# First layer: the last subchunk's convolutions on both column halves of the array

## The chip, the core and the metric

The kernel runs on one core of a Trainium2 chip. The core has a matrix engine (TensorE, PE in the profile; its weight loads are PEld), VectorE (DVE), ScalarE (ACT), GpSimd (POOL) and a queue engine, SyncE (SP), which here issues DMAs. Matmuls write to PSUM, an accumulator memory of 128 partitions, and only VectorE and ScalarE read it here. The metric is the time of one execution on the device, in microseconds; the time before is the median of three runs. The profile is of one more execution, which has a time of its own.

## What is computed

The input is 8 images of 56 x 56 pixels with 192 channels, float32. Four layers follow one another, each of the form x + layer(groupnorm(x)). The change touches the first, a gated Toeplitz convolution over rows and columns with 576 inner channels:

```
p = silu(x @ p_w.T + p_b)
q = silu(x @ q_w.T + q_b)
v = silu(x @ v_w.T + v_b)
qv = q * v
o1 = toeplitz(qv along a row,    a1)     # per channel, length 56
o2 = toeplitz(qv along a column, a2)
out = (p * (o1 + o2)) @ o_w.T + o_b
```

The tables a1 and a2 (112 values for each channel) come from two small MLPs over positions and a decay. The other layers are a windowed outlook attention, a gated attention unit and a recurrent scan; their code is the same before and after.

## The kernel before

**Tiling of the first layer** (`layer0`, line 136 on). The 576 inner channels are 9 subchunks of DS = 64 channels, numbered n = 9 b + s over the images b. Two subchunks make a chunk c; the last chunk, c = 4, has only one, s = 8, which the code calls the tail. Per image the loop at line 613 runs over the chunks.

**A subchunk's way.** `project` (line 283) forms q and v by matmuls over 7 image rows at a time in four steps g; ScalarE applies silu (line 310), and `multiply` (line 316) writes their product into the tile `qv`, on VectorE (line 319) and, partly transposed, on POOL and for the last step also on VectorE (line 325). `turn` (line 342) transposes qv on TensorE (line 352) and copies the outcome into the tiles `left` (`ol`, by VectorE) and `right` (`or`, by ScalarE), both at line 359. The other rows of these two tiles hold Toeplitz matrices of the channels, which `toeplitz` (line 265) loads for subchunk n + 2 when the convolutions of n are done, in four DMAs of 16 channels a side (line 275). `convolve` (line 363) then needs one matmul for each channel d, at line 376: 120 rows of `left` and `right` give the 56 x 56 sum o1 + o2 of that channel.

**The array's halves.** One such product has 64 columns of weights, half of the array's 128. For the ordinary subchunks a step q alternates between u = 0 and u = 1, so that channel d goes to PSUM partitions 0 to 63 and channel d + 32 to partitions 64 to 127; two steps of 32 products, with one copy of 120 partitions each into the tile `ot`. For the tail a step has u = 0 alone: four steps of 16 products on partitions 0 to 63, with one copy of 56 partitions each. Copies alternate: VectorE at line 392 for even q, ScalarE at line 390 for odd q. The tail's `ot` is laid out as [56, 56, 64], with the channel innermost.

**What follows the tail.** `post_tail` (line 491) forms the gate p of the last 64 channels (lines 503 and 510), transposes `ot` back (line 524), multiplies (line 530), applies the output matrix (lines 537 and 549) and adds into the accumulators (line 401). Its steps are mixed (`merge`, line 591) with the transposes `turn` of the next image's first two subchunks. Beside the tail's convolutions come the four steps of the next image's `project`, put ahead of them.

**Order and buffers.** In this layer the order on TensorE is the program's (`manual_schedule`, line 604); the other engines' queues are ordered by the compiler framework from dependencies. PSUM is used through `banks()` (line 159): a ring of four tiles of two banks each (line 157), so a step can start once the readers of the tile four steps back are done.

Of the kernel before, what the change touches and what calls it, by code (L numbers as in the profile page):

```python
# [17 lines left out]
H = 56  # L18
# [117 lines left out]
def layer0(cx, xin, xout, w, consts):  # L136
# [6 lines left out]
    tc, nc = cx.tc, cx.nc  # L143
# [7 lines left out]
    with ExitStack() as es:  # L151
# [7 lines left out]
        def banks():  # L159
            return cx.tile(psc, [128, 2, 512], "c")  # L160
# [22 lines left out]
        with ExitStack() as pes:  # L183
# [22 lines left out]
            for t in (1, 2):  # L206
# [13 lines left out]
                for i in range(3):  # L220
                    ps = banks()[0:32, 0, 0:NP]
# [4 lines left out]
                for s in range(NS):  # L226
                    ps = banks()[0:DS, 0, 0:NP]
# [135 lines left out]
        def convolve(n, ot):  # L363


            s = n % NS
            left, right = pairs[n % 2]
            tail = s == NS - 1

            def step(q):  # L370
                ps = banks()
                for k in range(2):
                    for v in range(8):
                        for u in range(1 if tail else 2):
                            d = q * 16 + 8 * k + v + u * 32
                            nc.tensor.matmul(  # L376
                                ps[u * 64 : (u + 1) * 64, k, v * H : (v + 1) * H],
                                left[:, d * H : d * H + 64],
                                right[:, d * H : (d + 1) * H],
                                start=True, stop=True, skip_group_check=True,  # L380
                            )
                if tail:
                    dst = ot[0:H, :, q * 16 : q * 16 + 16].rearrange("p h (k v) -> p h k v", k=2)
                    src = ps[0:H, :, 0 : 8 * H].rearrange("p k (v h) -> p h k v", h=H)
                else:
                    d0 = s % 4 * 32 + 16 * q
                    dst = ot[:, d0 : d0 + 16, :].rearrange("p (k v) h -> p k (v h)", k=2)
                    src = ps[0:120, :, 0 : 8 * H]
                if q % 2:
                    nc.scalar.copy(dst, src)  # L390
                else:
                    nc.vector.tensor_copy(dst, src)

            return [lambda q=q: step(q) for q in range(4 if tail else 2)]

        def add(m, j, x, ps):

# [213 lines left out]
        for b in range(B):  # L611
            more = b + 1 < B
            for c in range(NC):
# [17 lines left out]
                if c % 2 == 0:  # L631
                    ot = cx.tile(cp, [120, 128, H] if two else [H, H, DS], "ot")
                ahead = project(xn, c + 1) if two else project(nxt, 0) if more else []
                convs = []
                for m in (n, n + 1) if two else (n,):
                    *some, last = convolve(m, ot)
                    convs += some + [lambda m=m, last=last: (last(), toeplitz(m + 2))]
# [1397 lines left out]
```

## Time and profile before

| what | value |
|---|---|
| median of three runs | 4327.92 us (4323.49 to 4331.09) |
| the profiled execution | 4314.29 us, span 4312.5 us |
| mean granted TensorE clock | 0.975 |
| line 376, convolutions of the first layer | 9216 matmul records, 313.9 us of TensorE busy time |
| line 352, transposes of qv | 4032 records, 283.8 us |
| lines 294 and 301, projections | 2304 records, 428.8 and 233.2 us |
| copies of the tail, lines 392 and 390 | 16 on VectorE, 1080 ns each; 16 on ScalarE, 900 ns each |
| VectorE and ScalarE, share of the span | 54% and 41% |

How to read it: a busy time is the union of the intervals in which instructions of that group are in the engine, so overlapped matmuls count once; the mean duration of one is longer (223 ns at line 376), since their pipelines overlap. Each float32 product shows as two records; a transpose at line 352 shows as one. Eight images with 9 subchunks of 64 products make the 9216 records. In a list of groups or of the timeline, `out<-in` names the tiles, then partitions x elements, and the bracket holds the idle time before the instruction and what ended it.

### The profile page before, as it was taken

What the parts mean: (1) busy time and instruction counts of PE and PEld (TensorE: products, weight loads), DVE (VectorE), ACT (ScalarE), POOL (GpSimd) and SP (SyncE); (2) the same over time, 40 slices, a digit from 0 to 9 for tenths busy, and PEclk for the clock granted to TensorE, in tenths of its full rate; (3) what the DMA queues carried; (4) which work ended last, traced back from release to release, by engine and by line L of the source; (5) the groups of instructions that cost most, each with busy time, mean ns of one, the idle gap of its engine ahead of it and who ended that gap; (6) DMA issues with size and microseconds to landing.
All of it is one profiled execution on the core that took longest, in us unless ns stands there. A gap on an engine that the chain in (4) does not pass through costs nothing. (4 is left out here: it accounts for less than half of the span.)

```text
span 4312.5 us, 106542 instructions
## 1 busy us (share of the span) xinstructions
PE 4073.2 (94%) x46380; PEld 2680.7 (62%) x46380; DVE 2334.9 (54%) x3429; ACT 1782.9 (41%) x2052; POOL 1512.1 (35%) x1295
## 2 busy tenths in 40 slices
PE   6999999999999999999789999869998999998997
PEld 4666767676676666767456666524444555555997
DVE  4546555454656446554444444356665766664664
ACT  2334434334443343444234434223334555554664
POOL 3222232222322222232133333133333444444776
PEclk9999999999999999999889999879999999999999
DMA  6755242242523225232224344455547776664233
GB/s 137 142 106 142 61 113 61 70 104 61 133 71 98 53 69 128 61 94 73 72 65 116 97 107 104 126 165 171 171 140 175 170 177 154 156 152 113 76 111 93
DMA packets 379607, 484.14 MB, mean 112 GB/s; under 512 B 175780, under 2 KB 324372, under 8 KB 377236
## 3 DMA queue, kind: packets, MB, share of 16 engines
q1 hardware_dynamic: 373636, 466.97, 42.6%
q10 hardware_dynamic: 5504, 10.35, 0.8%
q8 instruction: 365, 5.98, 0.6%
q14 instruction: 102, 0.84, 0.1%
HBM read 321.49 MB, written 155.65 MB: 111 GB/s over the span
## 5 line engine op out<-in xcount | busy, mean ns | idle before, releaser
L325 POOL TENSOR_TENSOR qv<-s,s 128x392 f32<-128x392 f32 (+3 forms) x320 | 567.8, 1796 | 1471.8 <-ACT s L310 1471.5
L359 ACT COPY or<-c 56x1024 f32<-56x1024 f32 (+1 forms) x288 | 256.3, 901 | 442.7 <-DVE ol L359 433.1
L310 ACT ACTIVATE s<-c,bqv 128x784 f32<-128x784 f32 (+1 forms) x320 | 278.4, 911 | 378.5 <-PE c L301 184.2
L294 PE MATMUL c<-xa,wqv 128*128 128x392 f32 x1152 | 428.8, 513 | 4.3 <-DVE xa L49 2.7
L319 DVE TENSOR_TENSOR qv<-s,s 128x784 f32<-128x784 f32 (+1 forms) x160 | 200.8, 1255 | 261.2 <-ACT s L310 261.2
L359 DVE COPY ol<-c 56x1024 f32<-56x1024 f32 (+1 forms) x288 | 300.0, 1077 | 63.8 <-PE c L352 62.5
L376 PEld LDWEIGHTS c<-or,ol 120*64 120x64 f32 x9216 | 305.4, 138 | 37.2 <-issue 27.3
L376 PE MATMUL c<-or,ol 120*64 120x56 f32 x9216 | 313.9, 223 | 9.4 <-DMA ol<-ed 7.8
L294 PEld LDWEIGHTS c<-xa,wqv 128*128 128x128 f32 x1152 | 209.0, 192 | 174.6 <-issue 35.3
L352 PEld LDWEIGHTS c<-ident,qv 64*120 64x120 f32 x4032 | 257.3, 138 | 55.4 <-issue 35.1
L352 PE MATMUL c<-ident,qv 64*120 64x64 f32 x4032 | 283.8, 224 | 3.8 <-POOL qv L325 2.5
L1367 PE MATMUL v<-wvb,wa 128*128 128x512 f32 (+1 forms) x400 | 193.0, 615 | 49.2 <-ACT wa L1278 30.0
L301 PE MATMUL c<-xb,wqv 64*128 64x392 f32 x1152 | 233.2, 518 | 0.0
L427 ACT ACTIVATE s<-c,bp 128x448 f32<-128x448 f32 x224 | 129.9, 631 | 246.9 <-PE c L420 246.9
L1900 POOL TENSOR_TENSOR y<-y,s 128x448 f32<-128x448 f32 x168 | 185.1, 1102 | 93.1 <-ACT s L1879 93.1
L1869 PE MATMUL h<-ringv,am 128*64 128x57 f32 (+1 forms) x4400 | 192.6, 235 | 19.7 <-DVE ringv L1856 12.7
L458 PE MATMUL c<-po,wo 128*128 128x448 f32 x448 | 198.1, 564 | 7.0 <-DVE po L447 7.0
L1869 PE MATMUL h<-ringh,am 128*64 128x57 f32 (+1 forms) x4400 | 186.1, 231 | 8.8 <-DVE ringh L1875 8.8
L1378 ACT ACTIVATE vb<-sm 128x1024 f32<-128x1024 f32 (+1 forms) x100 | 103.7, 1038 | 214.2 <-issue 187.2
L413 PE MATMUL c<-xa,wp 128*128 128x224 f32 x896 | 190.3, 355 | 0.0
L401 DVE TENSOR_TENSOR acca<-c,acca 128x392 f32<-128x392 f32 (+1 forms) x120 | 67.3, 586 | 219.0 <-PE c L463 204.8
L1869 PEld LDWEIGHTS h<-ringv,am 128*64 128x64 f32 x4400 | 168.1, 140 | 23.0 <-DVE ringv L1856 13.6
(219 smaller groups left out, 7583.6 us busy)
## 6 DMA issues: line engine op xcount, KB each, us to landing
or<-tt SPq DMA_DIRECT2D x252, 196.0 KB
ol<-tt SPq DMA_DIRECT2D x252, 196.0 KB
vt<-v SPq DMA_DIRECT2D x56, 672.0 KB
v<-vb SPq DMA_DIRECT2D x96, 384.0 KB
x<-x SPq DMA_DIRECT2D x112, 168.0 KB
x<-x SPq DMA_DIRECT2D x112, 112.0 KB
bt<-bs SPq DMA_DIRECT2D x28, 448.0 KB
bs<-bs SPq DMA_DIRECT2D x56, 224.0 KB
```

The lines of the kernel that those rows point to most:

```text
L294: nc.tensor.matmul(ps[:, h, 0:n], wqv[0][:, j, :], xn[0][:, at : at + n], start=True, stop=False,)
L301: nc.tensor.matmul(ps[:, h, 0:n], wqv[1][rows, j, :], xn[1][rows, g * n : (g + 1) * n], start=False, stop=True,)
L310: nc.scalar.activation(t, ps[rows, :, 0:n], AF.Silu, bias=bqv[rows, j : j + 1])
L319: nc.vector.tensor_tensor(sub(qv[rows, 7 * g :, 64 + H - 1 :], (HH * 120, 2), (120, 7), (-1, H)), *(t.rearrange("p u (h w) -> p u h w", w= ...
L325: eng.tensor_tensor(sub(qv[rows, w0:, H - 1 - 7 * g - HH * u :], (120, w1 - w0), (-1, 7)), *(t[:, u].rearrange("p (h w) -> p w h", w=H)[:, ...
L352: nc.tensor.transpose(view(i // 8)[:, :, i % 8], qv[e : e + DS, i0 + i, :], ident[e : e + DS, e : e + DS],)
L359: copy(dst, src[rows])
L376: nc.tensor.matmul(ps[u * 64 : (u + 1) * 64, k, v * H : (v + 1) * H], left[:, d * H : d * H + 64], right[:, d * H : (d + 1) * H], start=Tr ...
L413: nc.tensor.matmul(out(u, h), wp[0][:, 2 * j + u, :], xn[0][:, at : at + n], start=(u == 0), stop=True, skip_group_check=True,)
L458: nc.tensor.matmul(pa, wo[:, 2 * j + u, 0:CA], pos[u], start=(u == 0), stop=(u == 1))
L1367: nc.tensor.matmul(out, x[:, at : at + n], wt, start=(k == 0), stop=(k == 1), skip_group_check=True,)
L1869: nc.tensor.matmul(ps[sides[c], y], am[a][:, m * CB : (m + 1) * CB], old[:, x], start=(n < 2), stop=True, skip_group_check=True,)
```

## The change

In the tail, a step's 32 products now alternate between both column halves, as in the ordinary subchunks, and there are two steps where there were four. Step q computes channels 16 q to 16 q + 15 on PSUM partitions 0 to 63 and channels 32 + 16 q to 47 + 16 q on partitions 64 to 127. The tile `ot` keeps its layout on partitions 0 to 55, so each step ends with two copies of 56 partitions: VectorE copies the lower half to where it was, and ScalarE copies the upper half from partitions 64 to 119 to partitions 0 to 55. Nothing is changed for the ordinary subchunks.

```diff
@@ -371,7 +371,7 @@
                 ps = banks()
                 for k in range(2):
                     for v in range(8):
-                        for u in range(1 if tail else 2):
+                        for u in range(2):
                             d = q * 16 + 8 * k + v + u * 32
                             nc.tensor.matmul(
                                 ps[u * 64 : (u + 1) * 64, k, v * H : (v + 1) * H],
@@ -380,8 +380,12 @@
                                 start=True, stop=True, skip_group_check=True,
                             )
                 if tail:
-                    dst = ot[0:H, :, q * 16 : q * 16 + 16].rearrange("p h (k v) -> p h k v", k=2)
-                    src = ps[0:H, :, 0 : 8 * H].rearrange("p k (v h) -> p h k v", h=H)
+                    for u, copy in enumerate((nc.vector.tensor_copy, nc.scalar.copy)):
+                        d0 = q * 16 + u * 32
+                        dst = ot[0:H, :, d0 : d0 + 16].rearrange("p h (k v) -> p h k v", k=2)
+                        src = ps[u * 64 : u * 64 + H, :, 0 : 8 * H]
+                        copy(dst, src.rearrange("p k (v h) -> p h k v", h=H))
+                    return
                 else:
                     d0 = s % 4 * 32 + 16 * q
                     dst = ot[:, d0 : d0 + 16, :].rearrange("p (k v) h -> p k (v h)", k=2)
@@ -391,7 +395,7 @@
                 else:
                     nc.vector.tensor_copy(dst, src)
 
-            return [lambda q=q: step(q) for q in range(4 if tail else 2)]
+            return [lambda q=q: step(q) for q in range(2)]
```

## The prediction

> **What bounds the kernel now.** I read the page's first two parts, then the waits of TensorE inside layer 0, then the timeline around the last subchunk's convolutions, and then the same stretch of time in each image. The page first: busy time of each engine, then the span in 40 slices.
>
> ```profile
> PE 4073.2 (94%) x46380; PEld 2680.7 (62%) x46380; DVE 2334.9 (54%) x3429; ACT 1782.9 (41%) x2052; POOL 1512.1 (35%) x1295
> ...
> PE   6999999999999999999789999869998999998997
> PEclk9999999999999999999889999879999999999999
> ```
>
> TensorE (PE) is busy 94% of the span, and layer 0, which ends near 2116 us (slices 1 to 20), shows nines after its first slice. Next, who TensorE waits for inside layer 0 (70 to 2116 us; total, times, longest):
>
> ```profile
> PE c L376 <- DMA ol<-ed: 7.8, 1, 7.8
> PE c L458 <- DVE po L447: 7.0, 8, 0.9
> PE c L537 <- DVE s L530: 3.3, 6, 2.1
> PE c L549 <- ACT or L359: 2.9, 5, 0.6
> ```
>
> These and three smaller rows make 26.3 us in 2046. So in this layer TensorE's own sequence is the time, and a matmul that goes saves its slot as long as nobody else becomes late. Now the timeline of the stage that changes, in image 0 (start, duration, engine, line, operation, count, idle before it):
>
> ```profile
> 319.91 7.67 PE L376 MATMUL c<-or,ol 120*64 120x56 f32 x128
> 321.17 0.53 DVE L325 TENSOR_TENSOR qv<-s,s 128x196 f32<-128x196 f32 x1 [3.35 <-ACT s L310]
> 321.61 1.66 DVE L319 TENSOR_TENSOR qv<-s,s 128x784 f32<-128x784 f32 x1
> 323.19 1.20 DVE L325 TENSOR_TENSOR qv<-s,s 128x196 f32<-128x196 f32 x1
> 323.88 0.90 ACT L390 COPY ot<-c 56x896 f32<-56x896 f32 x1 [2.75 <-PE c L376]
> 324.32 1.07 DVE L392 COPY ot<-c 56x896 f32<-56x896 f32 x1
> 327.51 1.15 PE L352 MATMUL c<-ident,qv 64*120 64x64 f32 x16
> 328.70 1.22 DVE L359 COPY ol<-c 56x1024 f32<-56x1024 f32 x1 [1.87 <-PE c L352]
> 329.95 1.01 ACT L359 COPY or<-c 56x1024 f32<-56x1024 f32 x1 [1.44 <-DVE ol L359]
> 332.08 2.35 DVE L359 COPY ol<-c 56x1024 f32<-56x1024 f32 x2 [2.15 <-PE c L352]
> 332.83 1.03 PE L524 MATMUL c<-ident,ot 56*128 56x56 f32 x14
> 337.05 1.04 DVE L401 TENSOR_TENSOR acca<-c,acca 128x392 f32<-128x392 f32 x2 [1.75 <-PE c L537]
> ```
>
> The tail's 64 products (128 records: each float32 product leaves two) take from 319.91 to 327.51, and TensorE then goes on at once. The price of both forms, from the busy table of four stretches (length; busy time and count of PE, weight load, VectorE, ScalarE and POOL; granted clock; DMA share and GB/s): two tails, the four steps of two ordinary subchunks, and one lone ordinary step:
>
> ```profile
> 319.91:327.51 7.60, 7.60 (x130) 7.54 (x129) 5.32 (x5) 2.12 (x3) 3.61 (x3) 1.00 0.47 127
> 2093.42:2100.87 7.45, 7.45 (x129) 7.45 (x129) 2.16 (x2) 0.90 (x1) 0.00 (x0) 1.00 0.01 2
> 364.59:372.20 7.61, 7.61 (x258) 7.55 (x257) 5.38 (x5) 2.14 (x3) 3.78 (x3) 1.00 0.64 172
> 494.45:496.45 2.00, 2.00 (x66) 1.94 (x64) 0.00 (x0) 1.97 (x3) 0.00 (x0) 1.00 0.08 26
> ```
>
> The third stretch has 256 records of the same operand shape in the time in which the tail has 128: products that alternate between the two column halves cost half each. The trace has eight tails, of 7.60 us to the next instruction in seven images and 7.45 in the last.
>
> [...] the ordinary steps need 7.61 / 256 = 30 ns a record, the tail 7.60 / 128 = 59 ns. [...] here copies are 1.08 us (VectorE) and 0.90 us (ScalarE), before as after. [...] at 328.70 VectorE copies one half of a tile's partitions, ScalarE's copy of the other half starts at 329.95, just after VectorE's end at 329.92, and is put down to it. I take that order for the two new copies of one tile as well.
>
> **The change part by part.**
> (1) Products. Nothing goes and nothing is added: 64 products, 128 records an image. The order moves so that the two column halves alternate, 4 steps of 16 becoming 2 of 32. At 30 ns a record that is 128 x 7.61 / 256 = 3.81 us where 7.60 were. Gain 3.79 us in seven images and 7.45 - 3.81 = 3.64 in the last: 26.5 + 3.6 = 30.2 us. Bounds: the lone steps' 2.00 us each would make 4.00 us, a gain of 28.6 us; the record spacing without the change-over to the next line is nowhere under 29 ns, so no more than 31.
> (2) Copies. Still two on VectorE and two on ScalarE an image, of 56x896 each; what moves is when and in which order. Half of them now shift from partitions 64 up to 0 up. No copy of this line does that before; the nearest is L310, where ScalarE reads the upper 64 partitions of a tile and writes the lower: 911 ns for 64x784, the same as the 128x784 form. I take nothing; at worst the shift costs as much again, 0.90 us on ScalarE, which is covered as (3) shows.
> (3) The chain behind them, in image 0's clock. TensorE's two steps end at 321.8 and 323.72. VectorE is in its qv products until 324.39 in any case (if it takes a copy in between, they end 1.08 us later and the sum is the same). Its copies then end at 325.47 and 326.55, ScalarE's at about 326.4 and 327.5. TensorE goes on 3.79 us sooner: the first transposes (L352) at 323.72, the gate (L503, L510) at 324.81, two more transpose steps at 327.09 and 328.1, and the tail's back-transposes (L524) at 329.04. What each needs: the first transposes read rows 0 to 15 of qv, whose writers are VectorE's first product, done at 321.7, and the first of POOL's two (2.74 us together from 321.28), done near 322.65; the tile they take is freed by ScalarE's activations, done at 321.14. The second transpose step takes the tile of the first convolution step, free at 326.4 against 327.09, and qv, done at 324.4; the third the tile of the second, free at 327.5 against 328.1. L524 needs ot, ready at 327.5, and the tile of the first transposes: VectorE copies that at 326.55 to 327.77, ScalarE until 328.8, against 329.04. Every margin is positive but small, 0.2 to 0.7 us. I take 0.05 us an image for semaphores and bound it by 0 and 1 us.
> (4) What VectorE finds next. It arrives 1.7 us late against TensorE's new clock, and the rows above show its idle times before that matters: 1.87 us at 328.70, 2.15 at 332.08 and 1.75 at 337.05. The lateness is gone by the second; from 337 on VectorE is busy to 364 without a pause of note, so without those gaps all of the gain would be in danger.
> (5) Toeplitz loads (L275, on SP). Tail steps free the columns d in another order: 0 to 15 and 32 to 47 after step one, the rest after step two. The loads are queued 0, 16, 32, 48, so the second waits for step two; all eight issues are then through at about 326 where it was 328.35. They serve the convolution of subchunk 10, some 40 us on: nothing. The image loads and stores behind them on SP hang on the same TensorE sequence and come 3.8 us earlier too.
> (6) Last image: no project step beside the tail. TensorE ends at 2097.2, copies at 2099.4, L524 would start at 2099.4: a stall of 0.1 at most. Layer 1 starts with loads that follow the last stores, which follow these sums, so it moves as a whole. Layers 1 to 3 hold the same instructions.
> Sum: 30.2 - 8 x 0.05 = 29.8, say 30 us. The profiled execution (4314.29 us, its span 4312.5) becomes 4284.3; the median shown, 13.6 us above it, 4327.9 - 30 = 4298.
>
> **The rivals.**
> *A, half the gain stays in the copies.* If VectorE and ScalarE are ordered worse than in (3), for instance strictly one after the other over all four copies, ot is ready at 324.39 + 2 x (1.08 + 0.90) = 328.35 and the first transposes' tile, at the back of that queue, at 330.6. L524 then stalls 1.6 us, and what hangs on it (L530, L401) loses as much before VectorE's saturated stretch. 7 x (1.6 to 2) = 11 to 14 us lost: 4298 + 13 = 4311. For it: the margins of (3). Against: in the present tail ScalarE's copy (323.88 to 324.78) overlaps VectorE's (324.32 to 325.39) though both write ot.
> *B, no change.* VectorE is the bound of the stretch after the tail: busy 31.44 of the 37.08 us from 327.51 to 364.59. If its queue alone set the pace, all goes back: 4328. Against: the three gaps, and TensorE's waits for it there of 0.24 us.
> *C, slower: the granted clock.* [...] The place is all of layer 0, 2046 us at a mean clock of 0.99; 0.01 of it is worth 20 us, so from a loss of 0.015 on the gain is gone, and at 0.97 it is 41 us lost against 30 won: 4339. For it: stretches after two tails show 0.95, and slices of layer 1 and 2 eights and a seven. Against: eight of nine subchunks already run in pairs, at 1.00.
>
> **How the numbers follow.** Forecast 0.78, A 0.11, B 0.05, C 0.06. The forecast's own ends: 31 us and 24 us (28.6 less 0.6 an image) give 4297 to 4304, and the spread of the three runs, 4323 to 4331, adds 4 either side. The range takes in A's cost: 4289 to 4314. About 0.2% (8.6 us) is what a measurement of this kernel can tell from no change; forecast and A lie beyond it: faster 0.89, same 0.05, slower 0.06.
>
> **What would show it.** Step (1): L376 records of the tails at 30 ns, eight stretches of 3.8 us. Step (3): L352 following at once after them, and ScalarE's second copy of a step starting as VectorE's ends. Step (4): VectorE idle before 337 in image 0's old clock, less than now; the distance from one tail to the next convolution 40.9 us where it is 44.68. Wrong would be: a TensorE wait at L352 or L524 over 1 us in each image (A), the same 44.68 (B), or clocks under 0.98 in layer 0 (C).

## The result and the profile after

The changed kernel takes 4297.84 us in the median of four runs (4294.82 to 4299.32), the kernel before 4325.88 in four (the three runs above and one more): the ratio is 0.9931, with a 95% interval of 0.9917 to 0.9945, so 28 us less. The forecast was 4298. The profiled execution took 4297.32 us with a span of 4295.5, where the prediction had 4284.3 for it; that gap of 13 us has a section of its own below.

The tail first. From the busy table of stretches of the changed kernel (length; busy time and count of PE, weight load, VectorE, ScalarE and POOL; granted clock; DMA share and GB/s), an ordinary tail and the last one, and below them the stretch from a tail's start to the next convolution and from a tail to the next tail:

```profile
577.76:581.64 3.88, 3.88 (x131) 3.82 (x129) 2.62 (x3) 1.22 (x2) 3.38 (x3) 1.00 0.16 47
...
2075.78:2079.55 3.77, 3.77 (x127) 3.77 (x129) 1.08 (x1) 0.47 (x1) 0.00 (x0) 1.00 0.02 4
...
577.76:618.72 40.96, 39.89 (x398) 24.19 (x397) 37.20 (x55) 17.71 (x21) 14.45 (x9) 1.00 0.73 192
...
577.76:829.27 251.51, 249.38 (x2574) 170.89 (x2573) 139.96 (x189) 101.14 (x124) 70.72 (x41) 1.00 0.35 88
```

The kernel before, same stretches:

```profile
319.91:364.59 44.68, 43.61 (x398) 27.92 (x396) 36.75 (x55) 17.71 (x21) 14.49 (x9) 1.00 0.67 175
...
1088.01:1343.24 255.23, 253.09 (x2574) 174.59 (x2573) 139.11 (x189) 101.22 (x124) 70.70 (x41) 1.00 0.34 86
```

A tail went from 7.60 to 3.88 us. The stretch to the next convolution went from 44.68 to 40.96 and a whole image from 255.23 to 251.51: all three by the same 3.72 us. (Both images are the shortest of their profile; others that ran at full clock throughout take up to 255.57 us before and 251.77 after.) Nothing of it was given back inside the image. VectorE's busy time did not fall with it, so the stretch behind the tail is now denser for VectorE (37.20 of 40.96 us, before 36.75 of 44.68).

The chain behind the tail, image 0 of the changed kernel in its timeline (start, duration, engine, line, operation, count, idle before it); lines past 387 are shifted by four against the kernel before:

```profile
324.14 3.94 PE L376 MATMUL c<-or,ol 120*64 120x56 f32 x128
...
327.45 1.23 DVE L325 TENSOR_TENSOR qv<-s,s 128x196 f32<-128x196 f32 x1
...
328.01 1.15 PE L352 MATMUL c<-ident,qv 64*120 64x64 f32 x16
...
328.61 2.07 DVE L387 COPY ot<-c 56x896 f32<-56x896 f32 x2
...
329.71 1.90 ACT L387 COPY ot<-c 56x896 f32<-56x896 f32 x2 [4.35 <-DVE ot L387]
...
330.61 1.20 DVE L359 COPY ol<-c 56x1024 f32<-56x1024 f32 x1
...
331.84 1.01 ACT L359 COPY or<-c 56x1024 f32<-56x1024 f32 x1 [0.23 <-DVE ol L359]
...
332.58 2.35 DVE L359 COPY ol<-c 56x1024 f32<-56x1024 f32 x2 [0.77 <-PE c L352]
...
333.33 1.03 PE L528 MATMUL c<-ident,ot 56*128 56x56 f32 x14
...
337.55 1.04 DVE L405 TENSOR_TENSOR acca<-c,acca 128x392 f32<-128x392 f32 x2 [1.74 <-PE c L541]
```

ScalarE's first copy waits for VectorE's first, as the same tile's halves did at line 359. VectorE's idle times before its three next steps were 1.87, 2.15 and 1.75 us; they are now none, 0.77 and 1.74. The lateness of the copies is used up in the first two, and TensorE has no bracket anywhere in these rows.

### The profile page after: what moved, and what is told of

Read it like the earlier page. It is cut to its first block, busy times and chain, and to the rows that moved or that the text cites. A ratio compares the mean times of both kernels' runs of the same rounds, so it can differ in the third digit from the quotient of the medians.

```text
span 4295.5 us, 106533 instructions
## 1 busy us (share of the span) xinstructions
PE 4052.9 (94%) x46380; PEld 2655.7 (62%) x46380; DVE 2340.9 (54%) x3429; ACT 1781.9 (41%) x2052; POOL 1510.6 (35%) x1295
## 4 chain that ended last, share of the span: by engine, by line
PE 79%; DVE 6%; issue 5%; SPq 3%; DMA 3%; ACT 2%; POOL 1%; DVEq 0%; ACTq 0%; POOLq 0%
PE c L294 10%; PE c L376 6%; PE v L1371 6%; PE c L301 5%; PE c L462 4%; PE c L417 4%; PE c L924 4%; PE h L1873 4%; PE c L352 4%; PE y L959 3%; PE kv L1431 3%; PE c L442 3%; PE c L424 3%; DVE ol L359 2%; PE c L1583 2%
## 5 line engine op out<-in xcount | busy, mean ns | idle before, releaser
L376 PEld LDWEIGHTS c<-or,ol 120*64 120x64 f32 x9216 | 275.8, 139 | 39.5 <-issue 29.6
L376 PE MATMUL c<-or,ol 120*64 120x56 f32 x9216 | 284.5, 223 | 11.5 <-DMA ol<-ed 7.7
L1873 PEld LDWEIGHTS h<-ringv,am 128*64 128x64 f32 x4400 | 168.1, 140 | 22.9 <-DVE ringv L1860 12.7
```

The source lines that it names most:

```text
L376: nc.tensor.matmul(ps[u * 64 : (u + 1) * 64, k, v * H : (v + 1) * H], left[:, d * H : d * H + 64], right[:, d * H : (d + 1) * H], start=Tr ...
L1873: nc.tensor.matmul(ps[sides[c], y], am[a][:, m * CB : (m + 1) * CB], old[:, x], start=(n < 2), stop=True, skip_group_check=True,)
```

## The experiments

All times are medians, with the ratio to the kernel before run beside them and its 95% interval. "Image" is the distance from one tail's start to the next in the profile, taken from images without a half-clock window (a stretch of 3.413 us in which the record of granted clock shows half; more below). Such images of one profile differ by up to 0.5 us, with 18 products twice by up to 1.0.

| run | time, us | ratio | image, us |
|---|---|---|---|
| changed kernel | 4297.84 | 0.9931 (0.9917 to 0.9945) | 251.51 |
| the same again | 4303.27 | 0.9947 (0.9934 to 0.9959) | 251.52 |
| halves one after the other | 4318.57 | 0.9986 (0.9976 to 0.9996) | 254.9 |
| alternating in images 0 to 3 only | 4303.65 | 0.9953 (0.9939 to 0.9966) | 251.5, then 254.9 |
| tail copies all on ScalarE | 4299.95 | 0.9941 (0.9929 to 0.9953) | 251.51 |
| tail copies all on VectorE | 4310.67 | 0.9970 (0.9957 to 0.9982) | 252.8 |
| 18 products twice | 4306.93 | 0.9956 (0.9940 to 0.9972) | 252.55 |
| 18 products twice, again | 4304.85 | 0.9956 (0.9943 to 0.9970) | 252.57 |
| short copies to ScalarE | 4294.52 | 0.9931 (0.9918 to 0.9944) | 251.43 |
| all copies of two subchunks to ScalarE | 4294.36 | 0.9929 (0.9916 to 0.9941) | 251.4 |
| kernel before, again | 4325.80 | 1.0000 (0.9990 to 1.0011) | 255.4 |

### Is it the alternation?

```diff
-                for k in range(2):
-                    for v in range(8):
-                        for u in range(2):
+                kvu = [(k, v, u) for k in range(2) for v in range(8) for u in range(2)]
+                if tail:
+                    kvu.sort(key=lambda i: i[2])
```

> The changed kernel with one thing undone: in a tail step the 16 products of the lower half come one after the other, then the 16 of the upper half, instead of alternating. Two steps, two copies a step, as changed. If the gain is two products at once on the two halves of the array: tails back at about 7.6 us, time that of the kernel before, 4326 +- 6 us. If it is the fewer steps or the other copies: tails may be long but the time stays near 4298.

Time 4318.57 us. The changed kernel's two steps and its four copies are all there, and with the order of the products undone most of the gain is gone. The stretch of one tail in this kernel's busy table:

```profile
576.37:583.42 7.05, 7.05 (x131) 6.99 (x129) 4.31 (x4) 2.13 (x3) 3.67 (x3) 1.00 0.28 72
```

7.05 us, not the 7.60 that I expected, and the time lies 1.4 us under the 4320 to 4332 of the expectation. The start times of single records in the trace show what differs: within a run of one half they come 58 to 59 ns apart, as before, but at each of the three changes from one half to the other six records come in pairs 5 to 11 ns apart, with 47 to 53 ns between pairs. The trace doesn't name a record's half; I take such a pair to be one record of either half, run together over the border; that is my reading of the start times. The tail is 0.55 us shorter than before, and 8 x 0.55 = 4.4 us of the 6.7 us by which this kernel lies under the one before (1.7 to 10.4 by the interval of its ratio).

### Does it add up tail by tail?

The same edit, with `if tail and n >= 4 * NS`.

> The changed kernel with alternating products in the tails of images 0 to 3 only; in images 4 to 7 the products of each half come in one run, as in the first experiment (tails of 7.04 us). If the gain is a sum over tails: four tails at 3.88 and four at 7.04, so 4298 + 4 x 3.16 = 4310.6 us. If the gain came from somewhere else (start, copies, steps): near 4298 or near 4319.

Time 4303.65 us, nearer to the changed kernel than expected; beside the changed kernel's own second measurement of 4303.27 the times alone do not tell the two apart. Its profile does: one tail and one image of each kind.

```profile
822.58:826.46 3.88, 3.88 (x131) 3.82 (x129) 2.62 (x3) 1.22 (x2) 3.38 (x3) 1.00 0.18 49
1582.72:1589.76 7.04, 7.04 (x130) 6.98 (x128) 4.31 (x4) 2.13 (x3) 3.68 (x3) 1.00 0.27 75
822.58:1074.27 251.69, 249.54 (x2575) 171.01 (x2573) 139.42 (x189) 101.15 (x124) 71.59 (x41) 1.00 0.35 88
1582.72:1837.63 254.91, 252.75 (x2574) 174.18 (x2572) 140.06 (x189) 101.15 (x124) 70.70 (x41) 1.00 0.33 86
```

The tails differ by 3.16 us and the images by 3.2: the change's effect is local to its image. The kernel's time as a whole missed the forecast by 7 us. The changed kernel's own runs go from 4294.82 to 4306.07 us, so five runs don't settle a difference of this size; the adding up is shown by the profile and not by the times.

### How much room have the copies?

```diff
-                    for u, copy in enumerate((nc.vector.tensor_copy, nc.scalar.copy)):
+                    for u, copy in enumerate((nc.scalar.copy, nc.scalar.copy)):
```

> The changed kernel with all four tail copies of an image on ScalarE, none on VectorE. If the copies are covered on either engine: 4298 +- 4 us, tails 3.88 us. If VectorE's copies hold TensorE up after the tail: each image gains up to their 2.06 us, 4284 or so.

Time 4299.95 us, image 251.51 as in the changed kernel, although VectorE's busy time from tail to next convolution fell to 35.32 us. The copies are covered. The other way round, with VectorE for both:

> The changed kernel with all four tail copies on VectorE. If the margins of 0.2 to 0.7 us of the prediction are real, VectorE's queue ends 2.1 us later, the first transposes' tile comes free about 1.7 us after the tail's back-transposes could start, and seven images lose it: 4298 + 12 = 4310 us, with a TensorE wait of 1 to 2 us at line 528. If VectorE's idle time takes it all up: 4298 +- 4.

Time 4310.67 us against the 4310 expected. Image 4 in its timeline:

```profile
1346.86 4.40 DVE L387 COPY ot<-c 56x896 f32<-56x896 f32 x4
...
1351.29 3.48 DVE L359 COPY ol<-c 56x1024 f32<-56x1024 f32 x3
1351.38 1.02 PEld L352 LDWEIGHTS c<-ident,qv 64*120 64x120 f32 x16 [0.72 <-PE c L352]
1351.41 1.13 PE L352 MATMUL c<-ident,qv 64*120 64x64 f32 x16 [0.61 <-DVE ot L387]
...
1353.60 1.54 PE L507 MATMUL c<-xa,wp 128*64 128x392 f32 x8 [0.20 <-ACT or L359]
```

The four copies last from 1346.86 to 1351.26 in one row, VectorE's three copies for the transposes queue up behind them, and TensorE waits: 0.61 us for the tile of the tail's second step (line 352) and 0.20 us at line 507. From this tail to the next convolution it is 42.02 us where the changed kernel has 40.96, and the image 252.81. (Of the 1.06 us in this stretch 0.8 are the two waits; the rest shows as busy time of TensorE, 40.15 us for 39.89.) I had put 1.7 us at line 528; it came one step earlier, at the tile of the third transposes, and was 1.1 to 1.3 us. So the margins of the prediction are real: one more VectorE copy in each step, and they are gone. That the median met 4310 is in part luck: seven images at 1.1 to 1.3 us make 8 to 9 us and not the expected 12, and the granted clock was lower in these nine runs (0.972 in the mean, 0.974 in the nine of the changed kernel).

### Where 13 us of the profiled gain went

The two first profiles differ by 17.0 us, where the eight tails took away 29.7. The starts of the tails say where the 12.7 us between went.

- *Ahead of the first tail, 4.2 us.* It starts at 319.91 us before and at 324.14 after, and the change has not yet run then. TensorE stalls once for 2.25 us at line 376 in image 0, with no releaser in the trace, and has one more half-clock window (at 145 us). Such a stall, of 1.7 to 2.8 us, stands in six of the ten profiles of the changed kernel and its variants and in neither of the two of the kernel before; whether the change has a part in it is not shown.
- *From the first tail to the last, 4.2 us.* 1773.51 us became 1751.64, 21.9 less, where seven tails took 26.0.
- *From the last tail to the end, 4.3 us.* 2219.1 us became 2219.8, where the last tail should have taken 3.7 off.

The middle part is the clock. In the record of granted clock both kernels have windows of 3.413 us at half clock in the middle of layer 0. Such a window in the changed kernel, and the like stretch of the kernel before in an image without one:

```profile
848.36:851.78 3.42, 3.33 (x14) 1.46 (x11) 3.42 (x5) 2.29 (x3) 0.00 (x0) 0.50 0.81 239
```

```profile
343.28:346.69 3.41, 2.58 (x17) 1.00 (x18) 3.41 (x5) 2.13 (x3) 0.00 (x0) 1.00 0.60 194
```

Both lie on the output matmuls of the tail (lines 537 and 549, now 541 and 553), where TensorE at full clock has waits of 0.24, 0.59 and 0.24 us. In the window shown the eight output matmuls of line 541 take 2.98 us, in the other stretch the same eight (line 537) 1.59 us. From the clock of 0.50 and these two I estimate that a window costs at most half its length, 1.7 us. The images touched by a pair of them, 37.5 us apart, take 2.0 to 2.1 us longer: 257.28 for 255.23 in the kernel before, 253.65 for 251.51 after. The first of the pair costs only 0.4 us (41.39 us from tail to convolution for 40.96), since the waits of 0.24, 0.59 and 0.24 us vanish in it; the second falls on the next projection and costs the rest, 1.7 us.

```profile
575.15:832.43 257.28, 256.21 (x2574) 176.15 (x2572) 139.51 (x189) 101.23 (x124) 70.72 (x41) 0.99 0.33 86
```

```profile
829.27:870.66 41.39, 41.30 (x399) 24.79 (x397) 37.60 (x55) 17.71 (x21) 14.52 (x9) 0.96 0.73 193
...
829.27:1082.92 253.65, 252.49 (x2575) 172.28 (x2573) 139.88 (x189) 101.15 (x124) 71.61 (x41) 0.99 0.34 87
```

The first profile of the kernel before had the pair in two of its images, that of the changed kernel in four: two more pairs at 2.1 us are the 4.2 us of the middle part. Within a trace all changes of clock lie on one grid of 3.413 us: in the changed kernel windows start at 343.19, 848.36 and 1353.54 us, 148 steps of 3.4133 us apart each time. The two first profiles don't start at the same place of it: counted back from these starts, a line of the grid comes 1.86 us after the start of the span, and in the kernel before, by its window at 597.81 us, 0.48 us after. On such a grid an image of 255.23 us, 74.8 windows, begins at another place each time, and so does one of 251.51 (73.7). An image of 74.0 windows would not. I lengthened the tail to that:

```diff
+                if tail and q == 0:
+                    kvu = kvu[:18] + kvu
```

> The changed kernel with 18 products of the tail's first step computed twice (same outcome), 36 records at 30 ns = 1.07 us of TensorE a tail. It makes an image 252.58 us, which is 74.0 times 3.413 us, the length of the half-clock windows in the record of granted clock. If these windows come from a fixed grid that the image's period drifts against: the drift stops, so the pair of half-clock windows comes in no image (4298 + 8.6 - 8 = 4298 us) or in every image (4315). If they have nothing to do with the period: every second image still, 4306.5 us.

The profiled execution took 4296.90 us, its span 4295.1 with 8 x 1.05 = 8.4 us more work than the changed kernel's 4295.5, and no half-clock window between 300 and 2080 us. One of its images:

```profile
574.83:827.38 252.55, 250.43 (x2610) 171.94 (x2609) 139.92 (x189) 101.15 (x124) 70.74 (x41) 1.00 0.35 87
```

But its six times run from 4292.62 to 4317.29, and their median of 4306.93 is what the outcome without any tie to the period asked for (4306.5). The same kernel again:

> The changed kernel with 1.07 us of repeated products a tail, once more. Its image period of 252.56 us is 74 of the clock's windows, so an execution keeps its place on the grid: either no image or nearly every image has a half-clock window, and the times spread over more than 15 us, 4292 to 4317 as before. If the earlier spread was chance: within 5 us of 4306.

Median 4304.85 us; of eleven times six lie from 4298.88 to 4304.85 and five from 4312.01 to 4318.85, none between. The profiled execution, of 4303.78 us, is of the lower group and has one image with windows, near its end. Two groups look like "none or nearly every image", but no execution of the upper group was profiled, and three things speak against it. The first six times don't fall so (three lie from 4305.73 to 4308.19). The upper five have a mean granted clock of 0.9736, the lower six of 0.9753: as an estimate that is 0.0017 x 4310 x 2 = 15 us more of half clock, where pairs in seven images would be 48. And an image with a pair is 2.1 us longer, so the next one meets the grid 2.1 us further on, outside the stretch in which a pair comes (1.3 us wide, see below). So "nearly every image" was wrong, and what makes two groups stays open. The kernel before and the changed one, again:

> The kernel before, profiled once more. Its image without a half-clock window should again be 255.2 us from tail to tail; how many images are longer tells how much of the spread of its runs is the clock. If the number of such images is a property of the kernel: again two of six. If it depends on where an execution starts on the clock's grid: another number.

Median 4325.80 us, ten times from 4320.71 to 4335.31. Its profiled execution took 4324.48 us against 4314.29 of the first, with the windows in other places: a single one in three stretches and a pair at the end, 17.1 us of half clock between 300 and 2080 us where the first had 13.7.

> The changed kernel as it is, once more, beside the variants of this call. 4298 +- 4 us. If pairs of half-clock windows and the kernel's image period lock as the first profiles showed (a pair in every third image before, in every second after), the profile again shows about four pairs in the eight images.

Median 4303.27 us. No pair in every second image here: 13.7 us of half clock from 300 to 2080 us, where the first profile of the changed kernel had 27.3. The regular pattern of the first two profiles is not a property of the kernels; it depends on where an execution falls on the grid. Once there it can repeat: an image with a pair and one without are 253.65 + 251.51 = 505.16 us or 148.0 windows in the changed kernel, and one with and two without were 768.1 us or 225.0 windows in the kernel before.

All twelve profiles together show which place it is. Twice in an image TensorE does the transposes of two subchunks in one row (line 352, 112 of them, 7.4 us). Of 168 such rows behind the first tails 22 are followed at once by a half-clock window: all those in which a line of the grid falls 0.68 to 0.92 us after the start of the row, and no other. It is alike behind the tail: leaving out the kernel with all tail copies on VectorE and the two of the next section, which move the work there, a window comes in 22 of 63 images, all those in which a line of the grid falls 15.0 to 16.3 us after the tail's end, and in no other. Together these are 44 of the 54 half-clock windows of the twelve profiles between 300 and 2080 us.

### Can the rest of the waits go?

```diff
-                for t, rows, copy in ((left, T2, nc.vector.tensor_copy), (right, T1, nc.scalar.copy)):
+                own = nc.scalar.copy if s < 2 and ni == 8 else nc.vector.tensor_copy
+                for t, rows, copy in ((left, T2, own), (right, T1, nc.scalar.copy)):
```

> The changed kernel with one more move, in the stretch after the tail: the copies of the short transposes step (8 rows, 0.67 to 0.90 us) of subchunks 0 and 1 of each image go from VectorE to ScalarE for both sides. If VectorE's queue makes the TensorE waits left there (0.24, 0.59 and 0.24 us at lines 541, 553 and 352): they shrink by up to 1.07 us an image, 4298 - 4 to -7 = 4291 to 4294 us. If something else makes them: 4298.

The second takes `s < 2` alone as its condition.

> The changed kernel with all copies after transposes of subchunks 0 and 1 of each image on ScalarE, for both sides. If VectorE's queue is what is late after the tail and ScalarE has room (15.6 of 37.1 us busy there): the 1.07 us of waits an image go, 4290 us. If ScalarE becomes the bound, since a step of 1.05 us of transposes then needs 2 x 1.01 us of ScalarE copies: TensorE waits for tiles at lines 352 and 528, 1 to 2 us an image, 4306 to 4313.

Medians 4294.52 and 4294.36 us: the lowest of the study, though their intervals overlap those of the changed kernel, and an image is at most 0.1 us shorter. TensorE's waits in the changed kernel from 330 to 2060 us (total, times, longest), without the row of line 462 with 5.3 us:

```profile
PE c L553 <- ACT or L359: 1.8, 3, 0.6
PE c L541 <- DVE s L534: 0.7, 3, 0.2
PE c L352 <- ACT or L359: 0.7, 3, 0.2
```

and with all copies of the two subchunks on ScalarE, without the same row (now line 463, 5.2 us) and one of 0.2 us:

```profile
PE c L294 <- ACT or L360: 3.5, 7, 0.6
PE c L542 <- DVE s L535: 1.9, 7, 0.3
```

The stretch from tail to convolution has VectorE busy for 28.09 us instead of 37.20 and still takes 40.90 us. Relieved of a quarter of its work, VectorE hardly lets TensorE go sooner: ScalarE's copies are now what the next projection waits for (line 294). TensorE is idle for 40.90 - 39.88 = 1.02 us of the stretch, before for 40.96 - 39.89 = 1.07: the wait moved and hardly shrank. (The first list counts three and not seven, since four of its stretches have a half-clock window in which the waits vanish.) I do not count either kernel as faster than the changed one.

## Why the prediction was right, step by step

- *What bounds.* Right. TensorE's sequence is the time in layer 0: 3.72 us off the tail are 3.72 us off the image.
- *Step 1, products.* Right. Predicted 3.81 us a tail, measured 3.88 and 3.77; the sum is 7 x 3.72 + (7.45 - 3.77) = 29.7 us where I had 30.2. The order of the products is the cause: undone alone, it takes the image to 254.9 us.
- *Step 2, copies.* Right. ScalarE's 16 copies that shift from partition 64 to 0 take 902 ns each, before 900 without the shift; VectorE's 1070, before 1080. (The 1.90 us of two in one row of the timeline hold the wait between them.) I had taken nothing for the shift, and nothing is what the trace shows.
- *Step 3, the chain.* Right to 0.1 us. (The 0.05 us an image for semaphores was an allowance of mine, and no run measured it alone.) Counted from the tail's start, VectorE's copies were to end at 6.64 us and did at 6.54, ScalarE's at 7.6 and did at 7.47, line 524 was to start at 9.13 and did (as line 528) at 9.19. The margins are shown by the kernel with all copies on VectorE, which lost 1.1 to 1.3 us an image and, against the two measurements of the changed kernel, 7 to 13 us in all. The place of that loss I had a step too late.
- *Step 4, VectorE's gaps.* Right: the gaps at the first two steps took it up, the third stayed at 1.74 us.
- *Steps 5 and 6.* The loads on SP never show as a TensorE wait beside the one of image 0, there before and after (7.8 and 7.7 us). Layers 1 to 3 did not move by themselves: from the last tail's start to the end it is 2219.1 us before and 2219.8 after in the first profiles, 2218 to 2226 in all others. The 3.7 us of the last tail are not to be seen in that spread.
- *Sum, and where it failed.* The median, 4297.84 us against 4298, is closer than the method deserves: the second measurement gave 4303.27. The step "the profiled execution becomes 4284.3; the median shown, 13.6 us above it" was wrong. It took the distance between one profiled execution and the median as fixed, and it is chance: profiled executions of the kernel before took 4314.29 and 4324.48, of the changed one 4297.32 and 4303.27, and of 69 other executions of the kernel before one alone was faster than 4314.29. The 12.7 us that the first two profiles lack are those of the list above: 4.2 ahead of the first tail, 4.2 in two more pairs of half-clock windows, 4.3 behind the last tail. In the mean of all runs the kernel before takes 4326.2 us (69 runs) and the changed one 4299.9 (9 runs), 26.3 us less, where the tails give 29.7. Whether the difference is chance, the last tail, the stall or the clock, the runs don't show.
- *Rivals.* A, half the gain left in the copies: no. The kernel with all copies on VectorE shows the kind of wait that A meant, but at line 352 and not at 524, and smaller: 1.1 to 1.3 us an image where A had 1.6 to 2. B, no change: no. C, a lower granted clock, which I had supposed might come of denser work: not in the size that C needs. Layer 0 (70 us to its end) has a granted clock of 0.99 in both profiles of either kernel, where C was to show under 0.98, and the half-clock time varies as much between two executions of one kernel (13.7 and 27.3 us after, from 300 to 2080 us) as between the kernels. A small fall is not excluded: the mean of a run's granted clock is 0.9745 before (65 runs) and 0.9737 after (9 runs), by estimate 3 to 4 us at most.

## What to carry to other kernels

Where products use half of the matrix array's columns, let neighbours in program order go to different halves: here it was the order, not the number of products in a step, that made them run two at a time (a tail of 3.88 us alternating, of 7.05 with the same two steps and one half after the other). Before counting such a gain, follow the copies behind it one by one against the sped-up engine: here they fitted by an estimated 0.2 to 0.7 us, and two copies an image moved to the busier engine took a third of the gain back (1.1 to 1.3 of 3.72 us). And compare like stretches of two profiles (a tail, an image), not two single executions: here the stretch gave 3.72 us to within some tenths, where the executions' times were off by 13 us.

## What the runs showed of the hardware that was not expected

- With alternating halves two records start 6 to 7 ns apart and the next pair 58 to 59 ns after the first: a pair costs what one alone does. At a border between runs of one half and of the other, six records start in such pairs too, 5 to 11 ns apart (the kernel with the halves one after the other).
- A ScalarE copy of 56x896 float32 from PSUM takes the same 0.90 us whether it shifts from partition 64 to 0 or not.
- TensorE, whose records fill 2.58 of 3.41 us behind the tail, with no wait over 0.59 us, still gets half clock there for single windows of 3.413 us. Whether it does goes by the place on the grid, without an exception in these profiles: behind the tail where a line of the grid falls 15.0 to 16.3 us after its end (22 of 63 images), behind a row of 112 transposes where one falls 0.68 to 0.92 us after its start (22 of 168 rows). An image with a pair of windows is 2.0 to 2.1 us longer. What the clock reacts to, the transposes or something else, was not tested.
- 1.07 us more work an image, chosen so that the image is a whole number of these windows, cost nothing in one execution (4296.90 us), which kept its place on the grid and had no half-clock window from 300 to 2080 us. Other executions took up to 4318.85 us, and why is open.
